# A fourth block product of the experts' second layer by the second level, with two sets of sums

## The chip, the cores and the metric

The kernel runs on one core of one Trainium2 chip. The metric is the time of one execution in device microseconds (us), as the median of several runs. The profile is one further execution, recorded by the hardware profiler.

## The reference

The computation is one transformer block in float32. An attention layer (not touched here) is followed by a mixture-of-experts layer:

```python
B, T, C = x.shape                            # 8, 1024, 512
cap = max(1, int(T / E * CAPACITY_FACTOR))   # 160 rows for each batch entry and expert
probs = jax.nn.softmax(x @ Wr + br, axis=-1)
topk_p, topk_e = jax.lax.top_k(probs, K)     # 2 of 8 experts for each token
...
buf = buf.reshape(E, B * cap, C)             # 8 experts, 1280 rows, 512
h = jax.nn.relu(jnp.einsum('enc,ech->enh', buf, W1) + b1[:, None, :])   # 2048 hidden
y = jnp.einsum('enh,ehc->enc', h, W2) + b2[:, None, :]
...
return y_tok.reshape(B, T, K, C).sum(axis=2) # weighted by topk_p, summed
```

The change lies in the second einsum, h times W2.

## The kernel before

Each expert's 1280 rows are worked on in two parts, the `chunks`: first 768 rows (`nh` = 3, even `i`), then 512 (`nh` = 2, odd `i`). There are 16 chunks. The rows of a chunk are two halves of `nh` blocks of 128.

Both layers multiply matrices by a scheme of Strassen's kind: the operands are cut in 2 x 2 quarters, sums and differences of quarters are formed on VectorE, and seven products take the place of eight. In layer 1 (`layer1`, class `Hidden`) `q` runs over eight stages. Each stage does seven products p1 to p7 on TensorE (L1239), copies and activates on ScalarE (L1249 copies p1 out of PSUM, L1255 p5, L1259 p6, L1272 p7; L1278 to L1281 are the activations) and forms sums on VectorE (L1264, L1268, L1273, L1282 to L1285). p6 adds to the PSUM bank of p1, so it has to wait for L1249. `mix_w1` (L1214) forms four sums of each stage's weights W1 one stage ahead; p5 needs the first of them, t1. The tile `hid` holds seven parts: the left operands of layer 2's seven products. `mix_w2` (L1067 to L1070) forms the sums of an expert's W2 during its 768-row chunk, one of eight steps in a stage from `q` = 2 on, and the last two steps after the stages (`rest(mixes)`).

Layer 2 of chunk 0 is done block by block by `layer2` (matmuls at L1340). From chunk 1 on, blocks 0 and 1 of both halves are done together by `layer2_quad`. A plain product there (`product`, L1473) is 16 matmuls of 256 columns. Three of the seven products, those of (hidden part, weight) (1, 1), (2, 2) and (3, 6), are cut once more ("the second level"): `mix(n)` forms eight sums of quarters on VectorE (L1422 to L1429, 512 elements in each partition), and `second_level` does seven chains of four matmuls of 128 columns each (L1439). The order in `layer2_quad` is: sums 0, plain products 0/0 and 4/3, second level 0, sums 1, plain product 5/4, second level 1, y1 gated and sent, sums 2, plain product 6/5, second level 2, y2 gated and sent. In a 768-row chunk `layer2` does the third block after that (L1340).

The results are scaled by the routing weight on ScalarE (`gate`, L1310) and added to the rows of the output in DRAM by indirect DMAs that GpSimd issues (`send`, L1315). The generator `aside` is the gather of the next chunk's rows: after two steps that only load, each step transposes one row tile into `xe` (L1175), and the last also forms four sums (L1185 to L1188); in `layer2` it is asked for one step at each product. `mix_next` is `mix_w1` for stage 0 of the next chunk. `rows_ahead` fetches row tiles (L1097 on GpSimd) and stores them with SyncE (L1108), between the loads of W1 (L1045).

TensorE, ScalarE, VectorE and SyncE run their instructions in the order in which the program writes them (`manual_schedule`); no planner moves them. The order of the Python statements is thus the order of each queue. PSUM offers the expert stage six banks (`ps_p`); the tiles for y come from the pool `yp` with four buffers.

Of the kernel before, what the change touches and what calls it, by code (L numbers as in the profile page):

```python
# [2 lines left out]

# [18 lines left out]
P = 128  # L22
# [51 lines left out]
def preln_attn_moe_kernel(  # L74
# [103 lines left out]
            vec_in[i * NCH : (i + 1) * NCH, :], v.rearrange("(c h) d -> c (h d)", h=HPC)  # L178
        )
    load_x(0)  # L180
    ident = const.tile([P, P], F32, name="ident")
    make_identity(nc, ident)
    base_first = qkt.tile([P, 2, S], F32, name="qk_base")
    t = xmp.tile([P, NTT, D], F32, name="x_mid").rearrange("p (i t) d -> p i (t d)", i=2)
# [1140 lines left out]
    def new_y():  # L1325
        y = pools["yp"].tile([P, D], F32, name="y")
        return y, y[:, :DC], y[:, DC:]

    def layer2(i, block, hid, aside):

        e = chunks[i][0]
        ws = w2_tiles[e]
        cols = slice(block * P, (block + 1) * P)

        def bank():
            return pools["ps_p"].tile([P, 512], F32, name="ps_p")[:, :DC]

        def product(ps, part, weight, first, last):
            for k in range(NHQ):
                nc.tensor.matmul(  # L1340
                    ps, lhsT=hid[:, k, part, cols], rhs=ws[weight][:, k, :],
                    start=first and k == 0, stop=last and k == NHQ - 1, skip_group_check=True,
                )
            next(aside, None)

        gate, send = outputs(i, block)
        (y1, y11, y12), (y2, y21, y22) = new_y(), new_y()
        low, high = b2_tiles[e][:, :DC], b2_tiles[e][:, DC:]

        def side_product():  # L1350
            side = bank()
            product(side, 1, 1, True, True)
            TT(y11, y11, side, ALU.add)

        plain_first = i == 0 and block == 0
        top = bank()
        product(top, 0, 0, True, False)
        nc.scalar.copy(y11, top)
        if plain_first:
            side_product()  # L1360
        mid = bank()
        product(mid, 4, 3, True, False)
        nc.scalar.copy(y22, mid)
        product(top, 5, 4, False, False)
        nc.scalar.copy(y12, top)
        if not plain_first:
            side_product()
            product(top, 6, 5, False, False)
            TT(y22, y22, top, ALU.add)
        product(mid, 2, 2, False, True)  # L1370
        TT(y12, y12, mid, ALU.add)
        TT(y1, y1, b2_tiles[e], ALU.add)
        gate(0, y1)
        send(0, y1)
        if plain_first:
            product(top, 6, 5, False, False)
            TT(y22, y22, top, ALU.add)
        TT(y22, y22, high, ALU.add)
        gate(1, y22)
        product(top, 3, 6, False, True)  # L1380
        TT(y21, top, low, ALU.add)
        gate(1, y21)
        send(1, y2)

    def places(i, hid):

# [12 lines left out]
            for k in range(count)  # L1399
        ]  # L1400

    SECOND = [(1, 1), (2, 2), (3, 6)]

    def layer2_quad(i, hid, aside, before_last):

        e = chunks[i][0]
        ws = w2_tiles[e]
        free = places(i, hid)
        low, high = b2_tiles[e][:, :DC], b2_tiles[e][:, DC:]
        two = range(2)  # L1410

        def split(t, part_of):
            return [[part_of(t[:, 4 * k : 4 * k + 4], c) for c in two] for k in two]

        def mix(n):
            part, weight = SECOND[n]
            a = split(hid, lambda t, c: t[:, :, part, c * P : (c + 1) * P])
            b = split(ws[weight], lambda t, c: t[:, :, c * P : (c + 1) * P])
            (a11, a21), (a12, a22) = a
            (b11, b12), (b21, b22) = b  # L1420
            t1, t2, t3, t4, s2, s3, s4 = free[:7]
            TT(t1, b12, b11, ALU.subtract)  # L1422
            TT(s3, a11, a21, ALU.subtract)
            TT(a21, a21, a22, ALU.add)
            TT(t2, b22, t1, ALU.subtract)
            TT(s2, a21, a11, ALU.subtract)
            TT(t3, b22, b12, ALU.subtract)
            TT(s4, a12, s2, ALU.subtract)
            TT(t4, b21, t2, ALU.subtract)  # L1429
            return (  # L1430
                (a11, b11), (a12, b21), (s4, b22), (a22, t4), (a21, t1), (s2, t2), (s3, t3)
            )

        def bank():
            return pools["ps_p"].tile([P, 512], F32, name="ps_p")

        def chain(ps, pair, first):
            for k in range(4):
                nc.tensor.matmul(  # L1439
                    ps, lhsT=pair[0][:, k, :], rhs=pair[1][:, k, :], start=first and k == 0,  # L1440
                    stop=k == 3, skip_group_check=True,
                )

        def second_level(n, pairs):
            m1, m2, m3, m4, m5, m6, m7 = pairs
            c = free[7 + n]
            c11, c12, c21, c22 = (c[:, k, :] for k in range(4))
            u, v, z = (bank()[:, :P] for _ in range(3))
            chain(u, m1, True)
            nc.scalar.copy(c11, u)  # L1450
            next(aside, None) if n < 2 else None
            chain(v, m5, True)
            nc.scalar.copy(c21, v)
            chain(u, m6, False)
            nc.scalar.copy(c12, u)
            chain(z, m2, True)
            TT(c11, c11, z, ALU.add)
            chain(u, m7, False)
            nc.scalar.copy(c22, u)
            chain(v, m3, False)  # L1460
            TT(c22, c22, c21, ALU.add)
            TT(c12, c12, v, ALU.add)
            chain(u, m4, False)
            nc.scalar.copy(c21, u)
            return [c[:, 2 * b : 2 * b + 2, :] for b in two]

        def as_pair(t):
            return t.rearrange("p (c n) -> p c n", n=P)

        def product(ps, part, weight, first, last):  # L1470
            for b in two:
                for k in range(NHQ):
# [4 lines left out]
                        skip_group_check=True,  # L1477
                    )

        gate, send = zip(*(outputs(i, b) for b in two))  # L1480
        some(2, aside)
        pairs = mix(0)
        top, mid = bank(), bank()
        of = lambda ps, b: ps[:, b * DC : (b + 1) * DC]
        y1, y11, y12 = zip(*(new_y() for _ in two))
        product(top, 0, 0, True, False)
        for b in two:
            nc.scalar.copy(y11[b], of(top, b))
        next(aside, None)
        product(mid, 4, 3, True, True)  # L1490
        some(3, aside)
        c = second_level(0, pairs)
        for b in two:
            TT(as_pair(y11[b]), as_pair(y11[b]), c[b], ALU.add)
        pairs = mix(1)
        product(top, 5, 4, False, False)
        for b in two:
            nc.scalar.copy(y12[b], of(top, b))
            TT(y12[b], y12[b], of(mid, b), ALU.add)
        c = second_level(1, pairs)  # L1500
        for b in two:
            TT(as_pair(y12[b]), as_pair(y12[b]), c[b], ALU.add)
        y2, y21, y22 = zip(*(new_y() for _ in two))
        for b in two:
            nc.scalar.copy(y22[b], of(mid, b))
        for b in two:
            TT(y1[b], y1[b], b2_tiles[e], ALU.add)
            gate[b](0, y1[b])
            send[b](0, y1[b])
        pairs = mix(2)  # L1510
        product(top, 6, 5, False, True)
        for b in two:
            TT(y22[b], y22[b], of(top, b), ALU.add)
            TT(y21[b], of(top, b), low, ALU.add)
            TT(y22[b], y22[b], high, ALU.add)
        before_last()
        c = second_level(2, pairs)
        for b in two:
            TT(as_pair(y21[b]), as_pair(y21[b]), c[b], ALU.add)
            gate[b](1, y22[b])  # L1520
            gate[b](1, y21[b])
            send[b](1, y2[b])


    AHEAD = 2
# [17 lines left out]
    def experts(ending):  # L1543
# [5 lines left out]
        for i, (e, j0, nh) in enumerate(chunks):  # L1549
            parts, box = box[0], [None]  # L1550
            hid = pools["hp"].tile([P, NHQ, 7, HALF], F32, name="hid")
            tiles = None
            ahead = rows_ahead(i + 1) if i and i + 1 < len(chunks) else iter(())
            for q in range(NHQ):
                if i or q != NHQ - AHEAD - 1:
# [4 lines left out]
                if i and q > 1:  # L1560
                    next(mixes, None)
                next(ahead, None)
                tiles = layer1(Hidden(i, q, parts, hid, [ending]), tiles, q == NHQ - 1)
                if i == 0 and q == NHQ // 2:
                    rest(ending)
                    to_router.close()
                    for name, bufs in (("w2p", 1), ("yp", 4), ("bp", 1)):
                        pools[name] = to_end.pool(name, bufs, reuse_waits="tile", **left)
                    load_ahead(NHQ - 1)
                    load_b2(0)  # L1570
# [15 lines left out]
                    mix_w1(i + 1, 0)  # L1586

            if i:
                layer2_quad(
                    i, hid, iter(()) if nh > 2 else aside, mix_next if nh == 2 else lambda: None  # L1590
                )
            for block in range(2 if i else 0, nh):
                if block == nh - 1:
                    mix_next()
                layer2(i, block, hid, aside)
            rest(aside)
            if i % 2 and e + 1 < E:
                load_b2(e + 1)
# [251 lines left out]
```

## Time and profile before

| What | us |
|---|---|
| median of 3 runs (lowest to highest) | 3210.43 (3210.02 to 3211.08) |
| profiled execution, its own time | 3195.52 |
| span of the profiled execution | 3193.8 |
| TensorE busy | 3122.6 |
| VectorE busy | 2209.3 |
| ScalarE busy | 1664.9 |

In profile lines PE is TensorE, PEld its weight loads, DVE VectorE, ACT ScalarE, POOL GpSimd and SP SyncE. `out<-in` are the program's names, "x" a number of instructions, and a bracket at the end of a timeline row tells how long the engine was idle before it and what ended that. One f32 matmul of the program appears as two records.

### The profile page before, as it was taken

To read this page: it belongs to the slowest core of one execution; us is meant where nothing else is said; L and a number is where in the kernel's file an instruction comes from. 1 tells how busy PE (TensorE), PEld (TensorE's weight loads), DVE (VectorE), ACT (ScalarE), POOL (GpSimd) and SP (SyncE) were. 2 spreads that over 40 slices of the span, in tenths; PEclk is the share of its full clock that TensorE was granted. 3 is DMA by queue.
4 is the path that set the end of the run, shared out by engine and by line. 5 is a ranking of instruction groups with operands and counts; after the bars stand their busy time and mean duration, and the time that the engine had idled before them with its cause. 6 is when DMAs were issued, how large, how long until landed. Compare 5 with 4: busy or idle time off the path is not lost.

```text
span 3193.8 us, 51293 instructions
## 1 busy us (share of the span) xinstructions
PE 3122.6 (98%) x19726; PEld 2145.4 (67%) x19726; DVE 2209.3 (69%) x4643; ACT 1664.9 (52%) x2554; POOL 426.8 (13%) x387
## 2 busy tenths in 40 slices
PE   5999999999999999999999999999999999999998
PEld 2444444444444444689698698698698698698687
DVE  8888878888788775637657657656657656656654
ACT  7888888888888885413423423323323323323322
POOL 3000202020111123411011011011011011011010
PEclk9999999999999999999999999999999999999999
DMA  5435454554645353423423433434433334334331
GB/s 166 147 100 165 120 159 132 148 140 138 184 108 159 80 166 88 141 60 98 147 57 98 140 62 103 130 63 112 120 70 110 115 74 114 107 80 116 96 60 21
DMA packets 288547, 358.72 MB, mean 112 GB/s; under 512 B 28376, under 2 KB 199088, under 8 KB 276272
## 3 DMA queue, kind: packets, MB, share of 16 engines
q1 hardware_dynamic: 264944, 312.20, 33.3%
q0 software_dynamic: 22912, 43.22, 7.4%
q8 instruction: 157, 2.57, 0.4%
q14 instruction: 86, 0.70, 0.1%
q10 hardware_dynamic: 448, 0.02, 0.0%
HBM read 207.02 MB, written 81.22 MB: 90 GB/s over the span
## 4 chain that ended last, share of the span: by engine, by line
PE 79%; DVE 3%; ACT 1%; issue 1%; DMA 0%; SPq 0%; POOLq 0%; DVEq 0%; ACTq 0%
PE ps_p L1239 30%; PE ps_p L1473 13%; PE av L717 9%; PE ps_p L1439 9%; PE ps_s L683 9%; PE ps_p L1340 7%; ACT e L703 1%; PE ps_s L215 1%; PE ps_s L697 1%; DVE qk_f L524 1%; DVE qk_r L447 0%; DVE xT L837 0%; DMA qk<-qk_r 0%; DVE v L447 0%; SPq L608 0%
## 5 line engine op out<-in xcount | busy, mean ns | idle before, releaser
L703 ACT ACTIVATE e<-ps_s 128x1024 f32<-128x1024 f32 (+1 forms) x640 | 569.6, 937 | 183.3 <-PE ps_s L683 110.2
L683 PE MATMUL ps_s<-qk 64*128 64x512 f32 (+3 forms) x3072 | 597.3, 505 | 28.6 <-DMA qk<-qk_r 12.4
L717 PE MATMUL av<-e,v 128*64 128x512 f32 (+3 forms) x3072 | 523.4, 490 | 0.0
L683 PEld LDWEIGHTS ps_s<-qk 64*128 64x128 f32 x3072 | 262.3, 187 | 216.1 <-issue 106.4
L717 PEld LDWEIGHTS av<-e,v 128*64 128x64 f32 x3072 | 200.5, 137 | 283.1 <-issue 267.1
L1239 PE MATMUL ps_p<-xe,w 128*128 128x256 f32 (+1 forms) x1024 | 317.6, 433 | 1.1 <-issue 1.1
L1239 PE MATMUL ps_p<-xe_s,t 128*128 128x256 f32 (+1 forms) x1024 | 317.7, 433 | 0.0
L1239 PE MATMUL ps_p<-xe,t 128*128 128x256 f32 (+1 forms) x1024 | 317.7, 433 | 0.0
L1315 POOL DMA_INDIRECT out_dram<-y,slots x80 | 127.1, 1589 | 1234.0 <-ACT y L1310 1016.6
L768 POOL DMA_INDIRECT slot_d<-token,slot x128 | 159.2, 1244 | 988.5 <-issue 612.3
L1282 DVE TENSOR_TENSOR hid<-hid 128x256 f32<-128x256 f32 (+1 forms) x128 | 64.0, 500 | 283.0 <-ACT hid L1280 283.0
L1239 PEld LDWEIGHTS ps_p<-xe_s,t 128*128 128x128 f32 x1024 | 193.8, 190 | 82.0 <-ACT hid L1249 2.5
L1239 PEld LDWEIGHTS ps_p<-xe,t 128*128 128x128 f32 x1024 | 194.2, 190 | 80.4 <-issue 0.4
L1239 PEld LDWEIGHTS ps_p<-xe,w 128*128 128x128 f32 x1024 | 193.7, 190 | 79.4 <-issue 1.2
L1473 PE MATMUL ps_p<-w_t,hid 128*128 128x256 f32 x960 | 212.2, 379 | 0.0
L1473 PE MATMUL ps_p<-w,hid 128*128 128x256 f32 x960 | 209.6, 379 | 0.0
L1473 PEld LDWEIGHTS ps_p<-w,hid 128*128 128x128 f32 x960 | 182.4, 190 | 26.3
L1473 PEld LDWEIGHTS ps_p<-w_t,hid 128*128 128x128 f32 x960 | 180.1, 190 | 23.2
L1239 PE MATMUL ps_p<-xe_s,w 128*128 128x256 f32 (+1 forms) x512 | 158.9, 433 | 0.6 <-ACT p L1255 0.6
L1249 ACT COPY hid<-ps_p 128x256 f32<-128x256 f32 (+1 forms) x128 | 54.2, 423 | 179.6 <-PE ps_p L1239 170.9
L1340 PE MATMUL ps_p<-w,hid 128*128 128x256 f32 x640 | 144.8, 381 | 2.5 <-DVE w L1068 2.5
L697 PEld LDWEIGHTS <-keys_b 64*128 64x128 bf16 x1536 | 80.8, 95 | 89.5 <-issue 71.5
(300 smaller groups left out, 4959.6 us busy)
## 6 DMA issues: line engine op xcount, KB each, us to landing
w<-in_L_ffn_W_dram SPq DMA_DIRECT2D x256, 256.0 KB, 3.4
w<-in_L_ffn_W_dram SPq DMA_DIRECT2D x64, 512.0 KB, 7.4
qk<-qk_c SPq DMA_DIRECT2D x124, 256.0 KB, 4.5
qk<-qk_r SPq DMA_DIRECT2D x120, 256.0 KB, 4.5
qk_base<-base_d SPq DMA_DIRECT2D x28, 1024.0 KB, 7.5
xn_d<-xn SPq DMA_DIRECT2D x72, 256.0 KB, 2.4
rows_d<-xg SPq DMA_DIRECT2D x70, 256.0 KB, 2.1
x_mid<-in_L_attn_x_dram SPq DMA_DIRECT2D x16, 1024.0 KB, 8.9
```

Of the source, the lines that this page charges most:

```text
L683: nc.tensor.matmul(ps[:, a, at : at + w], lhsT=pair[r, 1, kb * P : (kb + 1) * P], rhs=pair[r, 0, q0 : q0 + w], start=at == 0, stop=not own ...
L697: nc.tensor.matmul(out_, lhsT=keys_b[r, part, :], rhs=late, start=False, stop=part == 1, skip_group_check=True,)
L703: nc.scalar.activation(e, ps[:, :, :n], AF.Exp, scale=UNIT * UNIT / math.sqrt(2 * DH))
L717: nc.tensor.matmul(av[a * 64 : (a + 1) * 64, q0 - 512 * h :], lhsT=vt[:, kb, 2 * pr + a, :], rhs=es[i][:, a, at : at + w], start=kb == 0, ...
L768: queued = nc.gpsimd.indirect_dma_start(out=slot_d[b], out_offset=bass.IndirectOffsetOnAxis(ap=idx, axis=0), in_=src, in_offset=None,)
L1239: nc.tensor.matmul(ps, lhsT=weights[:, k, :], rhs=rows[:, k, :], start=first and k == 0, stop=last and k == 1, skip_group_check=True,)
L1249: nc.scalar.copy(self.blocks[0], self.top)
L1282: TT(g1, g3, h22, ALU.add)
L1315: ins = nc.gpsimd.indirect_dma_start(out=out, out_offset=bass.IndirectOffsetOnAxis(ap=meta[:, e, jj[r], 0:1], axis=0), in_=y, in_offset=No ...
L1340: nc.tensor.matmul(ps, lhsT=hid[:, k, part, cols], rhs=ws[weight][:, k, :], start=first and k == 0, stop=last and k == NHQ - 1, skip_group ...
L1439: nc.tensor.matmul(ps, lhsT=pair[0][:, k, :], rhs=pair[1][:, k, :], start=first and k == 0, stop=k == 3, skip_group_check=True,)
L1473: nc.tensor.matmul(ps[:, b * DC : (b + 1) * DC], lhsT=hid[:, k, part, b * P : (b + 1) * P], rhs=ws[weight][:, k, :], start=first and k == ...
```

## The change

The product of (hidden part 4, weight 3), called p5, is done by the second level too. The code of the second level becomes a class, `Second`, whose sums come in two halves: `weights()` forms the four sums of the weight quarters, `left()` the four of the hidden part; `both()` interleaves them. The keys 5, 2, 3, 4 stand for the operands (4, 3), (1, 1), (2, 2), (3, 6).

In the 512-row chunks there is room for two sets of sums (`rooms`), in columns of `hid` that those chunks don't use. There the weight sums of products 5 and 2 are formed in layer 1, two in each of the stages 3 to 6 (`early_sums`), their left sums at the start of layer 2, and the sums of 3 and 4 one product ahead; t1 overwrites a quarter of the weight. In the 768-row chunks all four products share one set.

In the 768-row chunks the third block's `layer2`, now a generator that yields after each product and the instructions that use it, is begun in between: its first two products run ahead of the last second-level product. In the 512-row chunks y1 is gated and sent after the last second-level product (`first_rows`). In the diff `extra` is `layer2(i, 2, hid)`, `last_part` means `nh == 2`, `ask` takes steps of `aside` in the 512-row chunks alone, and the yields of `layer2` are shown once. `yp` gets a fifth buffer, and `ident` moves to another pool.

```diff
-    ident = const.tile([P, P], F32, name="ident")
+    ident = own.tile([P, P], F32, name="ident")
...
-    def layer2(i, block, hid, aside):
+    def layer2(i, block, hid):
...
-            next(aside, None)
...
+        yield
...
+    class Second:
+        OPERANDS = {2: (1, 1), 3: (2, 2), 4: (3, 6), 5: (4, 3)}
...
+        def weights(self):
+            (b11, b12), (b21, b22) = self.b
+            t3, t2, t4 = self.w_room[:3]
+            t1 = self.w_room[3] if len(self.w_room) > 3 else b12
+            self.t = t1, t2, t3, t4
+            for to, x1, x2 in ((t3, b22, b12), (t1, b12, b11), (t2, b22, t1), (t4, b21, t2)):
+                TT(to, x1, x2, ALU.subtract)
+                yield
+
+        def left(self):
+            (a11, a21), (a12, a22) = self.a
+            s2, s3, s4 = self.a_room
+            self.s = s2, s3, s4
+            for to, x1, x2, op in (
+                (s3, a11, a21, ALU.subtract), (a21, a21, a22, ALU.add),
+                (s2, a21, a11, ALU.subtract), (s4, a12, s2, ALU.subtract),
+            ):
+                TT(to, x1, x2, op)
+                yield
+
+        def both(self):
+            w, a = self.weights(), self.left()
+            for gen, count in ((w, 2), (a, 2), (w, 1), (a, 1), (w, 1), (a, 1)):
+                some(count, gen)
...
+        def run(self, c, between=lambda: None):
...
+            chain(u, a11, b11, True)
+            nc.scalar.copy(c11, u)
+            between()
+            chain(v, a21, t1, True)
+            nc.scalar.copy(c21, v)
+            chain(u, s2, t2, False)
+            nc.scalar.copy(c12, u)
+            chain(z, a12, b21, True)
+            TT(c11, c11, z, ALU.add)
+            chain(u, s3, t3, False)
+            nc.scalar.copy(c22, u)
+            chain(v, s4, b22, False)
+            TT(c22, c22, c21, ALU.add)
+            TT(c12, c12, v, ALU.add)
+            chain(u, a22, t4, False)
+            nc.scalar.copy(c21, u)
...
+    def seconds(i, hid):
+        free = places(i, hid)
+        if chunks[i][2] == 2:
+            rooms = [(free[6 * n : 6 * n + 3], free[6 * n + 3 : 6 * n + 6]) for n in range(2)]
+            results = free[12:14]
+        else:
+            rooms = [(free[:4], free[4:7])] * 2
+            results = free[7:9]
+        return {w: Second(i, hid, w, *rooms[n % 2]) for n, w in enumerate((5, 2, 3, 4))}, results
...
+        ask(2)
+        if last_part:
+            rest(second[5].left())
+        else:
+            rest(second[5].weights())
+            rest(second[5].left())
         top = bank()
         y1, y11, y12 = zip(*(new_y() for _ in two))
         product(top, 0, 0, True, False)
         for b in two:
             nc.scalar.copy(y11[b], of(top, b))
-        next(aside, None)
-        product(mid, 4, 3, True, True)
-        some(3, aside)
-        c = second_level(0, pairs)
...
+        if last_part:
+            rest(second[2].left())
+        ask(2)
+        five = second[5].run(c5)
+        second[3 if last_part else 2].both()
+        ask()
         product(top, 5, 4, False, False)
         for b in two:
             nc.scalar.copy(y12[b], of(top, b))
-            TT(y12[b], y12[b], of(mid, b), ALU.add)
...
+        add_to(y12, five)
+        add_to(y11, second[2].run(c, ask))
+        second[4 if last_part else 3].both()
+        ask()
+        product(top, 6, 5, False, True)
...
+            TT(as_pair(y22[b]), as_pair(of(top, b)), five[b], ALU.add)
+            TT(y21[b], of(top, b), low, ALU.add)
+            TT(y22[b], y22[b], high, ALU.add)
+        add_to(y12, second[3].run(c, ask))
         for b in two:
             TT(y1[b], y1[b], b2_tiles[e], ALU.add)
...
+        if not last_part:
+            first_rows()
+            second[4].both()
+            some(2, extra)
+        before_last()
+        got = second[4].run(c5)
+        if last_part:
+            first_rows()
+        add_to(y21, got)
         for b in two:
-            TT(as_pair(y21[b]), as_pair(y21[b]), c[b], ALU.add)
-            gate[b](1, y22[b])
-            gate[b](1, y21[b])
+            gate[b](1, y2[b])
             send[b](1, y2[b])
...
+            if nh == 2:
+                second = seconds(i, hid)
+                early_sums = itertools.chain(second[0][5].weights(), second[0][2].weights())
...
+                if 2 < q < 7:
+                    some(2, early_sums)
...
-                    for name, bufs in (("w2p", 1), ("yp", 4), ("bp", 1)):
+                    for name, bufs in (("w2p", 1), ("yp", 5), ("bp", 1)):
...
+                if nh > 2:
+                    some(2, aside)
+                    for step in range(5):
+                        if step == 4:
+                            mix_next()
+                        next(extra)
+                        next(aside, None)
```

## The prediction

> **What bounds the kernel now.** I read the page's header and busy row first, then the chain that ended last in order of time, then the timelines of VectorE, ScalarE and GpSimd around the places that the change touches. The span is 3193.8 us; the profiled execution took 3195.5 us and the median of the runs is 3210.4 us, 14.9 more. I sum differences and add them to the median.
>
> ```profile
> PE 3122.6 (98%) x19726; PEld 2145.4 (67%) x19726; DVE 2209.3 (69%) x4643; ACT 1664.9 (52%) x2554; POOL 426.8 (13%) x387
> ```
>
> TensorE (PE) is busy 98% of the time. In the expert stage (from about 1440 us) the chain in order of time, whose columns are start, us and what, shows TensorE alone, without a gap, down to the last product:
>
> ```profile
> 2063.81 13.81 PE ps_p L1473 x64
> 2077.62 6.25 PE ps_p L1439 x56
> 2083.87 6.91 PE ps_p L1473 x32
> ...
> 2110.19 24.18 PE ps_p L1340 x112
> 2134.37 48.35 PE ps_p L1239 x224
> ...
> 3172.99 6.26 PE ps_p L1439 x56
> 3179.26 0.02 issue
> 3179.28 0.27 ACT hid L1464
> 3179.54 0.81 ACT y L1310 x2
> 3180.35 0.27 issue
> 3180.62 4.77 DMA out_dram<-y,slots
> ```
>
> An f32 matmul has two records, so a plain product of two row blocks (16 matmuls of 256 columns) is x32 and 6.91 us, and one by the second level (28 of 128 columns) x56 and 6.25 us. TensorE's time is the time, so whatever shortens it helps and whatever makes it wait costs in full. All waits it has now are zero here: the question is whether the new order keeps them zero.
>
> [...] 0.1116 us per record at 128 columns, 0.2159 at 256, more than half. So 7/8 of the columns cost 6.25/6.91 = 90%, not 87.5%. [...] in every VectorE timeline below the instructions stand in the order written. [...] The trace shows the like at 62.24 us: after 3.73 us of idleness (behind ACT's L703) eight matmuls of L683 took 3.44 us, against twenty in 5.04 us earlier.
>
> **The change, part by part.** There are 15 parts with a quad (chunks 1 to 15): seven of 768 rows (even) and eight of 512.
>
> 1. *TensorE work.* Product 4/3 goes from plain to second level: 15 x (6.91 - 6.25) = **-9.9 us**. Matmuls on the same tiles show the 0.1116 already.
>
> 2. *768 rows: p5's sums are late.* Before, 13.81 us of two plain products covered VectorE's sums; now one, 6.91 us, since the second product is itself the one that needs sums. VectorE's order there is: the last sums of the last hidden blocks, eight TTs of mix_w2 left over, then p5's four weight sums, then its four left sums.
>
> ```profile
> 2067.19 0.56 DVE L1285 TENSOR_TENSOR hid<-hid 128x384 f32<-128x384 f32 x1
> 2067.67 0.42 DVE L1067 TENSOR_TENSOR w_t<-w 128x256 f32<-128x256 f32 x1
> ...
> 2071.09 0.68 DVE L1422 TENSOR_TENSOR xe<-w 128x512 f32<-128x512 f32 x1
> 2071.69 0.69 DVE L1423 TENSOR_TENSOR xe<-hid 128x512 f32<-128x512 f32 x1
> 2072.41 0.69 DVE L1424 TENSOR_TENSOR hid<-hid 128x512 f32<-128x512 f32 x1
> ```
>
> The first sum can't start before 2071.09. One follows another after 0.60 us, (L1422 to L1423), or 0.72 if it has to wait for the one just before (L1423 to L1424, which overwrites what L1423 reads). So t3 2071.09, t1 2071.69, t2 2072.41, t4 2073.13, s3 2073.73, a21 2074.45 and ready at 2075.14. TensorE ends product 0/0 at 2063.81 + 6.91 = 2070.72, does the chain of a11 and b11 (6.25/7 = 0.89 us) and wants a21 with t1 at 2071.61. It waits to about 2075.2, 3.6 us. s2 and s4 (2075.9 and 2076.6) then arrive in time. Seven times 3.6: **+25.2 us**.
>
> 3. *768 to 512 rows.* The gather's steps and the mix_w1 for the next part now come a TT later each, because the products yield after their TT, and mix_w1 comes before step 4 instead of before all of the third block. Let T be the end of the last product. VectorE's order there becomes: L1371 and L1372 (the second-last product ends at T - 3.45), the fourth transpose, the four sums of xe, mix_w1's four, and only then the two TTs of y22 and y21. By durations and steps of before:
>
> ```profile
> 2127.89 1.10 DVE L1175 STREAM_TRANSPOSE xe<-xe_s 128x512 f32<-128x512 f32 x1
> 2129.02 0.69 DVE L1185 TENSOR_TENSOR xe_s<-xe 128x512 f32<-128x512 f32 x1
> ...
> 2131.20 0.69 DVE L1188 TENSOR_TENSOR xe_s<-xe,xe_s 128x512 f32<-128x512 f32 x1
> 2131.81 0.41 DVE L1371 TENSOR_TENSOR y<-y,ps_p 128x256 f32<-128x256 f32 x1
> ```
>
> L1371 T - 3.4, L1372 - 3.0, transpose - 2.3, sums from - 1.2 (0.73 each), mix_w1 from + 1.6, its t1 ready at + 2.0, y22 at + 3.1, y21 at + 3.4 to 3.8. The next part's p5 needs t1: a first wait of 1.2 us. Its p6 writes p1's bank, so it needs ScalarE's copy of p1 (L1249), and that is queued behind the two gates of y22 and y21: gates + 3.5 to 4.4, copy to + 4.7, p6 at about + 4.95. Now (T = 2134.37) it starts at 2135.93 = T + 1.56:
>
> ```profile
> 2134.86 0.51 ACT L1310 ACTIVATE y<-y,slots 128x256 f32<-128x256 f32 x1 [0.76 <-DVE y L1381]
> 2135.28 0.36 ACT L1249 COPY hid<-ps_p 128x256 f32<-128x256 f32 x1
> ...
> 2135.93 1.03 PE L1239 MATMUL ps_p<-xe_s,t 128*128 128x256 f32 x4
> ```
>
> That is 3.4 us in all, seven times: **+23.8 us**.
>
> 4. *512 to 768 rows.* first_rows() stands behind the last run, so four gates of 512 columns (0.62 us apart) instead of four of 256 (0.40) come ahead of p1's copy. That copy moves from T + 1.8 to T + 2.7 and ends at T + 3.15; p6 wants it at about T + 2.2. 1.0 us, seven times: **+7.0 us**.
>
> 5. *512 rows: runs 3 and 4 adjoin.* No plain product lies between. The last transpose and four sums of 960 ns delay VectorE's adds of run 3 to 1.4 us past its end; ScalarE's c21 copy waits for them and run 4's first copy for that: about 0.25 us, seven times: **+1.8 us**.
>
> 6. *The end.* The last part's y1 rows are sent after the last run too. GpSimd's sends follow each other only after the last has landed (start, us, and the idle time before it):
>
> ```profile
> 3174.05 1.56 POOL L1315 DMA_INDIRECT out_dram<-y,slots  x1 [3.98 <-issue]
> 3180.62 1.55 POOL L1315 DMA_INDIRECT out_dram<-y,slots  x1 [5.01 <-ACT y L1310]
> 3186.14 1.56 POOL L1315 DMA_INDIRECT out_dram<-y,slots  x1 [3.97 <-DMA out_dram<-y,slots]
> ```
>
> Before, two came after TensorE's end at 3179.26, and the span ended 14.5 us after it. Four at 5.55 us, the first at + 1.2, put the last at + 17.9 and the end, 7.7 us behind it, at + 25.5: **+11.0 us**.
>
> 7. *Costed at nothing.* The eight early sums in a 512-row part's layer 1, two per stage in four stages (1.3 us), lie in VectorE's idle 1.83 us per stage; without that cover, 0.1 to 0.3 us a stage that ScalarE's slack takes. The fourth run's three small TTs, the fifth y buffer and ident's place cost TensorE nothing. The four late sends hold GpSimd to about T + 21, where the second gather of the next rows starts at T + 19.85 now; behind it SyncE's row store and, behind that, a w1 load. Shifted by 2 to 4 us, the load goes from 2017.30 to 2021 and takes 3.4 us; VectorE wants it at 1991.56 + 4 x 9.03 = 2027.7. At worst 2 us a part if that cover is gone.
>
> Sum: -9.9 + 25.2 + 23.8 + 7.0 + 1.8 + 11.0 = +58.9, so **3269 us**. The unknown costs are 2 to 5, worked from queue orders and durations of before; the waits themselves exist in no trace yet. Below, none can be under zero: TensorE has no wait there to lose.
>
> **Rivals.**
> - *One of the two large waits is not there* (the sums are taken up earlier, or the gates don't hold the copy): +34 to +35, 3245 us. For it speaks only that TensorE never waits there now; against it the fixed orders. 0.13.
> - *The clock drops too.* A wait of 3.6 us is as long as the one at 62 us, after which eight matmuls lost 1.4 us and about 1.8 us went in all (granted clock 0.91 over 60 to 80 us). At each of the seven: +12.6, 3282 us. 0.12.
> - *Faster.* Only the TensorE work counts. The mechanism: VectorE has p5's a21 by 2071.61 instead of 2075.14, with its leftover mix_w2 behind or done, and the third block's late TTs no longer stand ahead of p1's copy. It decides once waits and tail together are under 9.9 us; since four late sends alone would cost 11.0, they would have to overlap as well. Then 3210.4 - 9.9 = 3200.5 us. With the tail alone, 3211.5, no change. Against it: the order of VectorE's queue and the send times. 0.04 and 0.03.
> - The change doing less than it says is excluded: TensorE's list has four second-level products per part.
>
> **How the numbers follow.** My case has 0.68 and gives 3269. Between 3240 (one large wait gone, small ones less) and 3288 (clock drops and 4 to 5 at 1.5 times) lies some 0.85. A measurement of this kernel can tell 0.2%, 6.4 us. Faster: 0.04; within: 0.03; slower: 0.93.
>
> **What would show it.** In the profile after, the chain should show second-level products of the 768-row parts' first run at 9.9 us instead of 6.25, the waits list TensorE for VectorE's hid (3.6 us, 7 times), and for ScalarE's L1250 copy 7 times at 3.4 in two pieces and 7 times at 1.0; the last four sends should follow TensorE's end. If the chain stays without gaps, 2 and 3 are wrong; if the tail is under 20 us, 6 is.

## The result, and the profile after

The changed kernel takes 3291.44 us (median of 6 runs, 3286.03 to 3294.05), before 3209.65 us on the same chip (6 runs, 3207.32 to 3211.08): 81.8 us more, a ratio of 1.0254 (95% interval 1.0240 to 1.0267). The profiled execution took 3290.79 us, its span 3289.1 us, its mean TensorE clock 0.986 (before 0.997).

The busy row of the page after:

```profile
PE 3148.0 (96%) x20086; PEld 2167.0 (66%) x20086; DVE 2310.1 (70%) x4808; ACT 1670.6 (51%) x2569; POOL 431.2 (13%) x387
```

TensorE was to become 9.9 us less busy and is 25.4 us busier (3122.6 before), in a span 95.3 us longer. So it waits now, and its instructions also take longer. Both can be read. The waits of TensorE on `ps_p`, from the list of waits after (us in total, times, longest):

```profile
PE ps_p L1463 <- DVE hid L1443: 25.3, 7, 3.6
PE ps_p L1240 <- ACT hid L1250: 21.6, 15, 6.7
...
PE ps_p L1240 <- DVE t L1215: 8.8, 7, 1.3
```

The first line is step 2 (p5's left sums at L1443), the third is step 3. In the TensorE timeline the 15 waits for L1250 of the second line are seven of 1.53 us (768 to 512 rows, step 3 too), seven of 0.59 (512 to 768 rows, step 4) and one of 6.7 in the first chunk. This is TensorE's timeline at the first boundary from 768 to 512 rows. The last product ends at T = 1680.08 (the next row's start is put a little ahead of that), and two waits follow, whose ends are 2.7 us apart:

```profile
1679.91 1.03 PE L1240 MATMUL ps_p<-xe,w 128*128 128x256 f32 x4
1682.20 1.13 PE L1240 MATMUL ps_p<-xe,t 128*128 128x256 f32 x4 [1.26 <-DVE t L1215]
1684.86 1.13 PE L1240 MATMUL ps_p<-xe_s,t 128*128 128x256 f32 x4 [1.53 <-ACT hid L1250]
```

p6 starts at T + 4.78; the forecast was T + 4.95.

What the list of waits does not show stands in the timeline right after a wait of step 2:

```profile
1610.28 1.05 PE L1463 MATMUL ps_p<-w,hid 128*128 128x128 f32 x8
1614.94 2.08 PE L1463 MATMUL ps_p<-xe,hid 128*128 128x128 f32 x8 [3.61 <-DVE hid L1443]
1616.82 1.91 PE L1463 MATMUL ps_p<-xe 128*128 128x128 f32 x8
...
1622.27 1.06 PE L1463 MATMUL ps_p<-xe,hid 128*128 128x128 f32 x8
```

Eight records of the same shape take 1.05 us before the wait, 2.08 and 1.91 after it, and 1.06 again 7 us later. For that time the array ran at half speed: the granted clock is 0.70 over 1610 to 1620 us.

The end, from GpSimd's timeline (first and last of the four sends):

```profile
3264.57 1.55 POOL L1316 DMA_INDIRECT out_dram<-y,slots  x1 [95.13 <-ACT y L1311]
...
3281.37 1.56 POOL L1316 DMA_INDIRECT out_dram<-y,slots  x1 [3.97 <-DMA out_dram<-y,slots]
```

TensorE ends at 3263.39, the span at 3289.1: 25.7 us, where before it was 14.5.

**The account.** From the start of the second chunk (1421.76 before, 1436.04 after) to TensorE's end the two traces differ by 1827.35 - 1757.50 = 69.9 us. Summed over stretches of 10 us, (1 - granted clock) x time is 0.0 us there before and 23.8 after. So 46.1 us are waits less saved work (forecast for steps 1 to 5: 47.9) and 23.8 us are clock. This split is good to some 2 us, since part of the half-speed time passed while TensorE was still waiting. With 11.2 us of tail (forecast 11.0) that is 81.1, against 81.8 by the medians. The other 14 us between the two profiles lie ahead of the second chunk: the first chunk starts 4.6 us later (1263.8 against 1259.2) and takes 9.7 us longer. The profiled execution of before was itself 14.1 us faster than the median above; more on this at the last experiment.

### The profile page after: what moved, and what is told of

Same layout as the page of the kernel before. It is cut to its first block, busy times and chain, and to the rows that moved or that the text cites. A ratio compares the mean times of both kernels' runs of the same rounds, so it can differ in the third digit from the quotient of the medians.

```text
span 3289.1 us, 52221 instructions
## 1 busy us (share of the span) xinstructions
PE 3148.0 (96%) x20086; PEld 2167.0 (66%) x20086; DVE 2310.1 (70%) x4808; ACT 1670.6 (51%) x2569; POOL 431.2 (13%) x387
## 4 chain that ended last, share of the span: by engine, by line
PE 72%; DVE 8%; ACT 2%; issue 1%; DMA 1%; another core or an unknown queue 0%; SPq 0%; POOLq 0%; DVEq 0%; ACTq 0%
PE ps_p L1240 29%; PE ps_p L1463 10%; PE av L718 9%; PE ps_s L684 8%; PE ps_p L1525 8%; PE ps_p L1341 6%; PE ps_s L216 1%; ACT y L1311 1%; ACT e L704 1%; PE ps_s L698 1%; DVE qk_f L525 1%; DVE xe L1432 1%; DVE qk_r L448 1%; DVE xe L1176 0%; DMA out_dram<-y,slots 0%
## 5 line engine op out<-in xcount | busy, mean ns | idle before, releaser
L1240 PE MATMUL ps_p<-xe_s,t 128*128 128x256 f32 (+1 forms) x1024 | 324.4, 440 | 21.6 <-ACT hid L1250 21.6
L1250 ACT COPY hid<-ps_p 128x256 f32<-128x256 f32 (+1 forms) x128 | 54.1, 423 | 186.0 <-PE ps_p L1240 165.3
L1341 PE MATMUL ps_p<-w,hid 128*128 128x256 f32 x640 | 144.8, 381 | 2.5 <-DVE w L1069 2.5
L1463 PE MATMUL ps_p<-w,hid 128*128 128x128 f32 x1104 | 145.6, 280 | 0.0
L1463 PEld LDWEIGHTS ps_p<-w,hid 128*128 128x128 f32 x1104 | 139.9, 197 | 2.3
L698 PEld LDWEIGHTS <-keys_b 64*128 64x128 bf16 x1536 | 81.1, 95 | 89.6 <-issue 71.8
```

The source lines that it names most:

```text
L698: nc.tensor.matmul(out_, lhsT=keys_b[r, part, :], rhs=late, start=False, stop=part == 1, skip_group_check=True,)
L1240: nc.tensor.matmul(ps, lhsT=weights[:, k, :], rhs=rows[:, k, :], start=first and k == 0, stop=last and k == 1, skip_group_check=True,)
L1250: nc.scalar.copy(self.blocks[0], self.top)
L1341: nc.tensor.matmul(ps, lhsT=hid[:, k, part, cols], rhs=ws[weight][:, k, :], start=first and k == 0, stop=last and k == NHQ - 1, skip_group ...
L1463: nc.tensor.matmul(ps, lhsT=left[:, k, :], rhs=right[:, k, :], start=first and k == 0, stop=k == 3, skip_group_check=True,)
```

## The experiments

**Theory:** the waits are those of the prediction, and a wait of TensorE costs twice, once itself and once more by the clock behind it if it is long enough. **Rivals:** the lower clock belongs to the whole run and not to the waits; or there is a fixed cost elsewhere (the fifth y buffer, `ident`, the first chunk). The groups of runs had different chips, on which before took 3195.0 us (first four), 3197.1 (next four) and 3206.3 (last four). So I compare ratios to before and turn their differences into us with 3200. For the changed kernel I take 1.0257, the mean of its two ratios (1.0254 and, in the last group, 1.0260).

### 1 to 4: the three causes one by one, and together

The first kernel takes the leftover `mix_w2` steps earlier:

```diff
                 if i and q > 1:
-                    next(mixes, None)
+                    some(2 if q in (4, 6) else 1, mixes)
```

> The changed kernel, with the two mix_w2 steps that were left over for the end of layer 1 taken in its stages instead, so that eight TTs less stand ahead of p5's sums on VectorE. Theory (a wait of TensorE costs itself and, where it is long enough, the clock after it): the seven waits of 3.6 us go (-25.3) and with them what the clock lost behind them (-13.3, from the 10-us stretches with a lowered clock there), so 3291.4 - 38.6 = 3253 us. Rival (the lower clock is a state of the whole run that has nothing to do with the waits): -25.3 alone, 3266 us, with the clock still lowered at five of those seven places. Second rival (something else is late there, such as ScalarE's copies or the weights): the waits shrink by less than half, above 3275 us.

Measured: ratio 1.0145 (1.0129 to 1.0160), 36 us less than the changed kernel. The seven waits for L1443 shrink from 3.6 us to 0.2. The rival asked for 25.3. In the expert stage 11.9 us of clock are still lost, all at the boundaries from 768 to 512 rows, whose waits are still there (7 x 1.26 and 7 x 1.53).

The second one restores the order at that boundary:

```diff
                     for step in range(5):
-                        if step == 4:
+                        if step == 0:
                             mix_next()
-                        next(extra)
                         next(aside, None)
+                        next(extra)
```

> The changed kernel, with mix_w1 for the next part ahead of the third block's products again, and the gather's step ahead of each product instead of behind it. Theory: the two waits at the start of the seven 512-row parts (1.3 for t1, 1.5 for ScalarE's copy) go, -19.6, and with them the clock lost there (-10.2 in the 10-us stretches), so 3291.4 - 29.8 = 3262 us; the waits of 3.6 us and the clock behind them stay. Rival (waits under 2 us don't lower the clock, it falls there for another reason): -19.6, 3272 us, with the clock still at 0.83 in the same places. Second rival (the order of the gates and the copy is not what makes p6 late): the L1250 wait of 1.5 stays, only the 1.3 goes, about 3280 us.

Measured: ratio 1.0153 (1.0139 to 1.0167), 33 us less. Both waits of that boundary are gone; 4.1 us remain for L1250, which are the seven of 0.6 at the other one. All the clock that is still lost, 15.3 us, lies behind the seven waits of 3.6 us.

The third one moves product 6/5 of the 512-row parts behind run 3, so that y1 is complete earlier:

```diff
+        if not last_part:
+            second[3].both()
+            rows_65()            # product 6/5 and its additions
         add_to(y12, second[3].run(c, ask))
...                               # b2 added to y1, gates and sends of y1
+        second[4].both()
+        if last_part:
+            rows_65()
         got = second[4].run(c5)
-        if last_part:
-            first_rows()
```

> The changed kernel, with product 6/5 behind run 3 in the 512-row parts, so that the first rows are complete, gated and sent ahead of run 4, and a plain product lies between runs 3 and 4 (runs 2 and 3 adjoin instead). Theory: the tail falls from 25.7 to about 14.5 us behind TensorE's end (-11), the seven waits of 0.6 us for ScalarE's copy go (-4), adjoining runs cost the same 0 to 0.3 us elsewhere: 3291.4 - 15 = 3276 us. Rival (the tail is set by how long the last sends take to land, not by how many are late): -4, 3287 us. Second rival (the sums of runs 2 and 3 come too late when the two adjoin, 1 us in each of 8 parts): 3284 us.

Measured: ratio 1.0202 (1.0188 to 1.0216), 18 us less. TensorE ends at 3241.6 and the span at 3255.6: the tail is 14.0 us. The seven waits of 0.6 are gone.

> The three edits together: p5 by the second level without any of the new waits. Theory: nothing is left but TensorE's saving, 9.9 us, with the clock as before: 3209.7 - 9.9 = 3200 us, up to 3207 by the sum of the three edits (3291.4 - 38.6 - 29.8 - 15), which would leave about 7 us in the first chunk, where the changed kernel also lost clock. Rival (clock independent of the waits): 3291.4 - 25.3 - 19.6 - 15 = 3231 us. Second rival (fixed cost somewhere else, such as the fifth y buffer or ident's place): no better than before, 3210 us or more, with the expert stage 10 us shorter and the stage ahead of it longer.

Measured: ratio 0.9989 (0.9982 to 0.9995), 3191.4 against 3195.0 us. Together the edits take 86 us off the changed kernel, apart 36 + 33 + 18 = 87, so they add up. The expert stage has no clock loss (0.0 us), although the fifth y buffer, `ident` and the first chunk are unchanged: neither rival holds. But of the 9.9 us saved only 3.6 arrive.

### 5: where the rest of the 9.9 us went

Two small waits remained in that kernel, 0.18 us for p5's a21 and 0.21 in each 512-row part's last run. The next kernel orders the sums differently:

```diff
-            rest(second[5].weights())
-            rest(second[5].left())
+            rest(second[5].in_turn())    # t3, t1, s3, a21, then t2, s2, t4, s4
...
+        some(4 if last_part else 0, sums)    # run 4's first four sums, ahead of b2's additions
```

> The three edits together as before, and in addition the two small waits that they leave are taken out: in the 768-row parts p5's sums in the order t3, t1, s3, a21, then the rest (a21 is ready 1.4 us earlier, the wait there was 0.2), in the 512-row parts run 4's first four sums ahead of the additions of b2 to y1 (there TensorE lost some 0.4). Theory (TensorE's work is all that is left): 7 x 0.2 + 7 x 0.4 = 4.2 us less than the kernel with the three edits, which had 3191.4; 3187 us, 8 less than before on this chip, a ratio of 0.9975. Rival (what is missing of the 9.9 us lies elsewhere): no change, ratio 0.999.

Measured: ratio 0.9985 (0.9979 to 0.9992), 3192.2 against 3197.1 us. That is the best of all kernels here, but only 1.3 us better than the last, which is less than the two intervals can tell apart. The first half worked: the wait for a21 is gone, and a 768-row part takes 0.65 us less than before, all that p5 saves. The second half missed. A 512-row part is only 0.19 us shorter than before: TensorE still waits 0.2 us for the first copy of run 4. That copy overwrites p5's result, which the additions of product 6/5 still have to read, and these stand behind the whole of run 4's sums on VectorE; b2's place among them changes nothing. TensorE's next eight records are slow as well, 1.16 us instead of 1.06 (see the last section). And since b2 is now added later, the last sends start later, and the tail is 16.2 us instead of 14.1. From the second chunk to TensorE's end this kernel takes 6.5 us less than before.

### 6 to 10: how long a wait has to be

Of the waits above these kernels have only the 0.2 us in the 512-row parts. In the seven 768-row parts idle repeats of a sum are put ahead on VectorE, so that TensorE waits for a chosen time and nothing else changes:

```diff
+            for _ in range(n):     # 2, 4, 6
+                TT(second[5].w_room[0], second[5].b[1][1], second[5].b[0][1], ALU.subtract)
             rest(second[5].weights())
             rest(second[5].left())
```

> A measured wait alone: the kernel without the small waits, but p5's sums of the seven 768-row parts again in the order weights, left sums, and with two idle repeats of the first of them ahead on VectorE, so that TensorE waits 0.2 + 2 x 0.61 = 1.4 us once in each. The waits are 10 us in all. Theory (the clock falls by degrees with how much of a short stretch TensorE was idle): some 0.4 us of clock for each, +13 over the kernel without waits, 3200 us. Rival [...]: +10, 3197 us.

> As the one before, with four repeats: one wait of 2.6 us in each of seven parts, 18.5 in all. Theory (by degrees): some 1.2 us of clock each, as in the changed kernel behind its two short waits of together 2.8, so +27 over the kernel without waits, 3214 us. Rival [...]: +18.5, 3205.5 us, and the clock at 1.00 in every stretch.

> As the one before, with six repeats: one wait of 3.9 us in each of seven parts, 27 in all. Both theories: some 2 us of clock each, as behind the waits of 3.6 in the changed kernel, so +41 over the kernel without waits, 3228 us. Rival (the clock there fell for another reason than the wait): +27, 3214 us.

The waits came out at 1.6, 3.1 and 4.5 us. The ratios are 1.0024 (1.0013 to 1.0035), 1.0093 (1.0078 to 1.0109) and 1.0138 (1.0122 to 1.0153), that is 12.5, 35 and 49 us over the kernel without waits. TensorE's timeline at the same place, first with the wait of 1.6:

```profile
1599.97 1.16 PE L1471 MATMUL ps_p<-xe,hid 128*128 128x128 f32 x8 [1.63 <-DVE hid L1443]
1600.97 1.06 PE L1471 MATMUL ps_p<-xe 128*128 128x128 f32 x8
```

and with the wait of 3.1:

```profile
1598.98 2.08 PE L1471 MATMUL ps_p<-xe,hid 128*128 128x128 f32 x8 [3.08 <-DVE hid L1443]
1600.85 1.61 PE L1471 MATMUL ps_p<-xe 128*128 128x128 f32 x8
```

After 1.6 us the records run at full speed, after 3.1 at half. My "by degrees" fails below (nothing at 1.6, where I had put 0.4), and the rival, the waits alone with the clock untouched, fails above (3.1 is enough in five of seven places).

The changed kernel's boundary has two short waits. To see whether they count together:

```diff
+            idle()
+            idle()                 # ahead of p5's sums
             rest(second[5].weights())
-            rest(second[5].left())
+            sums = second[5].left()
+            some(2, sums)
+            for _ in range(3):
+                idle()             # the same repeat, between a21 and s2
+            rest(sums)
```

> The kernel without waits (3192.2), with two repeats of a sum ahead of p5's and three more between a21 and s2 in the seven 768-row parts: TensorE waits 1.6 us for a21, does eight matmul records (0.9 us), and waits about 1.6 us again for s2. One wait of 1.6 cost 12.1 in seven parts and no clock; one of 3.1 cost 33.9, 12 of it beyond the waits. Theory (what counts is how much of a stretch of some us TensorE is idle, in one piece or two, so two short waits close together act as one of 3.2): 22.4 of waits and 12 of clock, 3227 us, as in the changed kernel behind its waits of 1.3 and 1.5. Rival (only an uninterrupted wait of about 3 us counts): 24, 3216 us, clock 1.00 throughout.

Measured: ratio 1.0092 (1.0075 to 1.0109), 34 us over the kernel without waits. Its timeline:

```profile
1606.83 1.16 PE L1471 MATMUL ps_p<-xe,hid 128*128 128x128 f32 x8 [1.63 <-DVE hid L1443]
1609.58 2.04 PE L1471 MATMUL ps_p<-xe 128*128 128x128 f32 x8 [1.59 <-DVE xe L1443]
```

Behind the first wait the eight records take 1.16 us, behind the second 2.04. The second wait is no longer than the one that did nothing when it was alone: the two act together.

The next kernel keeps the first wait (two repeats ahead of p5's sums) and puts the second at run 2:

```diff
+        if not last_part:
+            for _ in range(12):
+                TT(second[2].w_room[0], second[2].b[1][1], second[2].b[0][1], ALU.subtract)
         second[3 if last_part else 2].both()
```

> The same two waits of 1.6 us, 14 us apart: the first for p5's a21, the second one at run 2 (twelve repeats ahead of its sums, of which 5.7 us are slack). Theory: each is alone, no clock is lost, 24 us over the kernel without waits, 3216 us. Rival (the clock keeps account of idleness over a longer time than 14 us): 3227 us.

Measured: ratio 1.0131 (1.0114 to 1.0148), 47 us. This one doesn't answer its question: the second wait came out at 2.9 us instead of 1.6, and 31.9 us of waits with 11.9 of clock account for it, but for some 3 us. It does add two rows to the table below: a first wait of 1.6 us never lowered the clock, a wait of 2.9 us did in five of seven places.

### 11: the boundary with one wait

The kernel without waits, but of the edit at that boundary only the first half:

```diff
                     for step in range(5):
-                        if step == 4:
+                        if step == 0:
                             mix_next()
                         next(extra)
                         next(aside, None)
```

> The kernel without waits, but of the boundary from 768 to 512 rows only mix_w1 is ahead of the third block's products; the gather's step stays behind each product's additions as in the changed kernel. The waits for t1 go; y22 and y21 come about 1.6 us earlier than in the changed kernel, where p6 started at T + 4.8, so one wait of about 1.6 us for ScalarE's copy stays. Theory: 7 x 1.6 = 11, no clock lost, 3203 us. Rival (the clock falls at this boundary whatever the wait's length): 11 + 10, 3213 us. Second rival (mix_w1's place was the whole cause): 3192 us, no wait.

Measured: ratio 1.0027 (1.0016 to 1.0038), 13 us. TensorE at the boundary:

```profile
1672.74 1.13 PE L1240 MATMUL ps_p<-xe_s,t 128*128 128x256 f32 x4 [1.59 <-ACT hid L1250]
```

There is one wait of 1.6 us in each of seven places (11.2 in all) and no clock loss up to TensorE's end. So this boundary lowers the clock where both its waits are present and not where one is. p6 starts at T + 3.3 here, T + 4.8 in the changed kernel and T + 1.6 before: `mix_w1`'s place is one half of step 3, the gather's place the other.

### 12: the changed kernel again

Nothing is edited here.

> The changed kernel itself again, on the chip of these experiments. Theory (47.9 of waits less saved work, 11.1 of tail, 23.8 of clock; the first chunk's wait of 6.7 us in its first profile was that execution's own): 3196 + 83 = 3279 us, first hidden block of the second chunk at about 1422 us. Rival (the wait in the first chunk belongs to the change): the second chunk starts at 1436 us again, and 3290 us.

Measured: 3289.2 against 3206.3 us, 82.8 more, ratio 1.0260 (1.0243 to 1.0278); the sum in the expectation was 83. The absolute 3279 missed because before itself took 10 us more on this chip. The second chunk starts at 1428.1 us here, not at 1436.0, and the wait of 6.7 us in the first chunk is not there. In the other eleven kernels, with the same buffers and the same first chunk, the second chunk starts between 1420.8 and 1432.7, the late ones on the chip on which before is slower too. So the changed kernel is 83 us slower without that wait too; what causes the wait stays open.

### All waits in one table

A place has a loss if the clock falls to half between the wait's start and 1.5 us after its end. The loss is half of the half-speed time, in us.

| TensorE's wait in one place | places with a loss | loss in them |
|---|---|---|
| 0.6 us alone (changed kernel twice, 1st, 2nd) | 0 of 28 | |
| 1.6 us alone (6th, first of the 10th, 11th) | 0 of 21 | |
| 1.3 and 1.5, 2.7 apart (changed kernel twice, 1st, 3rd) | 18 of 28 | 1.7 or 3.4 |
| 1.6 and 1.6, 2.8 apart (9th) | 5 of 7 | 1.7 or 3.4 |
| 2.9 alone (second of the 10th) | 5 of 7 | 1.7 or 3.4 |
| 3.1 alone (7th) | 5 of 7 | 1.7 |
| 3.6 alone (changed kernel twice, 2nd, 3rd) | 24 of 28 | 1.7 or 3.4 |
| 4.5 alone (8th) | 7 of 7 | 1.7 or 3.4 |

The same wait at the same place of the program thus costs 0, 1.7 or 3.4 us of clock. The traces show what decides it. In each of them all changes of the clock lie, to within 0.01 us, on one grid with steps of 3.413 us. In the first profile of the changed kernel, for example, the clock falls at 1613.93, 1863.11 and 1931.37 us, which are 73 and 20 steps apart, and each time it stays low for one or two steps. So what counts is TensorE's idle time within one step. Here are two places of that profile, both with a wait of 3.6 us (stretch of time, its length, TensorE's busy time and matmul records, granted clock, the DMAs' share and GB/s):

```profile
1610.52:1613.93 3.41, 0.82 (x8) 1.00 0.00 0
1613.93:1617.35 3.42, 2.41 (x11) 0.50 0.00 0
1617.35:1620.76 3.41, 3.41 (x18) 0.50 0.00 0
...
2849.57:2852.98 3.41, 1.47 (x11) 1.00 0.00 0
2852.98:2856.39 3.41, 1.74 (x15) 1.00 0.00 0
2856.39:2859.80 3.41, 3.41 (x33) 1.00 0.00 0
```

In the first place TensorE is idle for 2.59 us (3.41 - 0.82) of one step, and the next two run at half speed. In the second the wait is split over two steps, 1.94 and 1.67 us, and the clock stays. From 70 us on, the 14 traces have 12,758 steps at full speed. Where TensorE was idle for less than 1.58 us of a step, the next one was never slower (0 of 12,646); from 2.0 us on it always was (71 of 71); in between it was in 10 of 41. This orders the table: a single wait of 1.6 us doesn't reach 2.0, one of 3.6 does unless it is split about evenly, one of 4.5 always does, and two short ones do where enough of both falls into one step. It is read from the traces afterwards; no run moved a wait along the grid to test it.

## Why the prediction was wrong, step by step

The sign and the mechanism of the waits were right, the clock was left out of the sum, and the time lies 3 us above the range. By its steps:

- **Step 1, TensorE's work.** Right: without any wait a 768-row part gains 0.65 us, the forecast's 6.91 - 6.25. The fifth kernel gains 6.5 of the 9.9 us up to TensorE's end; the rest is small waits in the 512-row parts. By the trace of before half the columns cost 52% of the time (0.1116 us per record against 0.2159).
- **Step 2, p5's sums late.** Right in length: seven waits of 3.6 us, down to 0.2 with the leftover `mix_w2` moved. Each costs 0.26 us beyond its length (last section), for which the sum had no term.
- **Step 3, 768 to 512 rows.** Right in size and in both its pieces, 1.26 and 1.53 us; p6 starts 0.17 us ahead of the forecast.
- **Step 4, 512 to 768 rows.** 0.6 us of wait instead of 1.0, plus the same 0.26.
- **Step 5, adjoining runs.** Runs 3 and 4 take 12.83 us together where two runs take 12.50: 0.3 us instead of 0.25.
- **Step 6, the tail.** Right: 25.7 us instead of 25.5, gone when y1 is sent earlier.
- **Step 7, costed at nothing.** Right: with steps 2 to 4 and 6 undone, no wait from it shows in the lists.

That the waits together came within 2 us of the forecast is in part luck: the missing 0.26 us at each wait of step 2 (1.8 in all) and steps 3 and 4, each about 1 us too large, pull opposite ways.

**What failed** is the term for the clock, which stood in the sum at nothing. The prediction knew it as the rival "The clock drops too", with seven drops of 1.8 us, 12.6 in all, and gave it a chance of 0.12 without an argument against it. What happened is 23.8 us in the first profile of the changed kernel and 27.3 in the second. Two things were wrong. The term counted only the waits of step 2, at a single size, where the loss is 1.7 or 3.4 (13.7 and 20.5 us in the two profiles). And it left out step 3's boundary, whose two short waits lower the clock together (10.2 and 6.8 us). 3269 + 23.8 is 3293, against 3291.4 measured.

The trace of before held evidence that the clock drops and that short waits add up. Its one wait of step 2's length, that at 62 us, had a drop behind it: one observation out of one was good ground for making the drop the main case. And in the first chunk it has two short waits close together:

```profile
1352.16 0.70 PE L1340 MATMUL ps_p<-w,hid 128*128 128x256 f32 x2 [1.01 <-DVE w L1068]
1353.87 1.20 PE L1340 MATMUL ps_p<-w,hid 128*128 128x256 f32 x2 [1.01 <-DVE w L1068]
```

They make 2.0 us of idleness between 1350.52 and 1353.93 us, one step of the grid, and from 1353.93 to 1360.76 the granted clock is 0.50.

## What to carry to other kernels

Where TensorE is the bound, cost each new wait at its length plus 0.26 us, which is what waits of 0.20 to 3.61 us cost here. Then ask how much idle time can fall within one step of the 3.413 us grid, adding up waits that lie close together. If it can reach 2.0 us (71 of 71 such steps here had a slow one behind them), add clock: here, over all places, 1.5 us on average after one wait of 2.9 to 3.1 us, 2.2 after 3.6 and 2.4 after 4.5. A saving of 0.66 us in each of fifteen places is worth what the queue orders around it cost: here three small ones (leftover sums, the place of the next weights' sums and of the gather, the place of the gates) turned 0.3% to be gained into 2.5% lost, and undoing them gave back a gain of 0.15%. So look at what stands last in VectorE's and ScalarE's queues at each boundary, and spread small sums over the stages instead of leaving a rest behind them.

## What the runs showed of the hardware

- A wait costs TensorE 0.26 us more than its length, also where it leaves the clock alone: with a wait of 1.63 us a 768-row part takes 144.05 us, without it 142.15. Where a wait of 3.61 us left the clock alone (changed kernel, 2849.99 to 2860.11 us), the seven chains take 10.12 us instead of 6.25. Of the 0.26 us, 0.10 us is that the first eight records behind the wait take 1.16 us instead of 1.06. The rest fits the 0.16 us by which the rows of an unbroken timeline overlap (1.06 us long, 0.89 apart) and which is missing at a wait.
- The clock changes on a grid of 3.413 us. From 70 us on it fell in these traces to half for the next step wherever TensorE was idle for 2.0 us or more of one, and never under 1.58 us. From the second chunk on it stayed low for one or two steps, 1.7 or 3.4 us of loss.
- How often that happens varies between two runs of one kernel, with where the waits fall on the grid: five and then seven of the seven waits of 3.6 us.
- The same first chunk ended at 1420.8 to 1436.0 us in different executions and on different chips, while its expert stage agrees within 1 us apart from the clock (1803.6 and 1802.6 us in the two profiles of the changed kernel).
